# A two-layer attention and MLP kernel: twelve copies out of PSUM go from ScalarE to VectorE

## The chip, the cores and the metric

The kernel runs on one core of a Trainium2 chip. The metric is the device time of one execution in microseconds, and the figure quoted is the median of the runs. A profile is one execution recorded by the hardware profiler; its times count from the start of the recorded span. Names of engines in the profile: PE is TensorE (PEld its weight loads), DVE is VectorE, ACT is ScalarE, POOL is GpSimd, and SP is SyncE, which issues most transfers.

## The reference

The input is one sequence of 2048 tokens with 256 features, all in fp32. Four steps follow one another, each added to its input:

```python
x = x + attn_a(layernorm(x), Wq, bq, Wk, bk, Wv, bv, Wo, bo)  # 16 heads of 16, 4 key heads, rotary angles
x = x + ffn(layernorm(x), gate_W_packed, gate_scales, up_W_packed, up_scales, down_W_packed, down_scales)
x = x + attn_b(layernorm(x), Wq, Wk, Wv, Wo)                  # 16 heads, 16 key heads, no angles
x = x + ffn(layernorm(x), ...)                                # the same weights again
```

Both attentions are causal with a softmax over the keys. The MLP has 2048 inner features, weights of 4 bits with one scale for every 32 inputs, and computes

```python
gelu = jnp.tanh(0.7978845608028654 * (gate + 0.044715 * gate ** 3)) * gate * 0.5 + gate * 0.5
out = jnp.einsum('tn,hn->th', gelu * up, Wd)
```

## The kernel before, in words

The tokens are worked on in four blocks of 512 (`NB` = 4, each of `NT` = 4 tiles of 128). The program writes down the order of every engine's instructions itself: each engine carries out its own list strictly as written, and semaphores make it wait for what the others still owe it. `weave` and `blend` deal the steps of several lists among one another, and each step puts its instructions on all the engines that it needs, at that place of each engine's list.

**Attention.** `Attention.run` goes through 16 units, one for each block b of queries and group g of four heads. A unit computes scores, exponentials and value sums for its block (`value_steps`) while the maxima of the next unit are found (`max_steps`). The last unit, (3, 3), has no next unit. In its place it takes the steps in `beside`, which are the preparation of the MLP's first block (`Mlp.prep_steps(0)`: layer norm, four normalised tiles `xn`, and then four turns). In the first attention it also takes a third of the steps that dequantise the MLP's weights (`dequant_steps`), which are spread over most of the first attention's units.

In the inner loop of a unit PE puts two pairs of scores of a 128-key tile into `ps_s` (three buffers; L856 adds the negated maxima, L865 the scores), ACT turns them into exponentials `e` (L873), and PE multiplies those by the values into the one bank `ps_av` (L911). When a unit's sums are whole, `end` copies `ps_av` to `o` in SBUF (L942), and `divide` turns `o` on PE into the bank `ps_m` (L949) and has DVE divide by the row sums (L954, L957). `end` and `divide` of a unit are not carried out in that unit, but after the first and third steps of the next one, so that `end` of unit (3, 2) stands near the start of the last unit. `end` of unit (3, 3) stands after the last unit's steps, and its `divide` among the first MLP products.

**The MLP's first block.** `turn(i)` in `Mlp.prep_steps` transposes the tile `xn` number i on PE (two 128x128 transposes, L1102) into `ps_m`, of which there is one buffer only, and copies the result to its place in `xnT` (L1103, 128x256). The next use of `ps_m` waits for that copy. The first MLP products (L1126) need all four places of block 0's `xnT`. The same function prepares blocks 1 to 3 during the MLP itself.

**Dequantising.** A piece of weights has six steps: `load` (a transfer of the codes by SP and eight of the scales issued by POOL, L339; two buffers each), `lowest` (POOL copies the low byte of each code, L344, one buffer), two of `move` (three small DVE operations each, L355 to L361) and two of `scaled` (one DVE operation each, L370). For the four pieces of the down weights `scaled` ends in a store to DRAM by SP (`wd_kept`, L399, from the one-buffer tile `dq_d`), and the MLP loads that whole again as `wd` (L1118).

Of the kernel before, what the change touches and what calls it, by code (L numbers as in the profile page):

```python
# [27 lines left out]
NG = NH // 4  # L28
# [3 lines left out]
NB = S // TB  # L32
# [48 lines left out]
def tile_hybrid_layers(  # L81
# [25 lines left out]
    nc = tc.nc  # L107
# [20 lines left out]
    def ps_m():  # L128
        return psum.tile([P, 512], F32, tag="m", name="ps_m")
# [158 lines left out]
    def layernorm_steps(xb, held):  # L288


        def one(i):
            if i == 0:
                held["sums"] = small.tile([P, NT, 6], F32, tag="stats", name="stats")
                held["mv"] = small.tile([P, NT, 2], F32, tag="mv", name="mv")
            nc.vector.bn_stats(held["sums"][:, i, :], xb[:, i, :])
            nc.vector.bn_aggr(held["mv"][:, i, :], held["sums"][:, i, :])

        def root():
            ve = small.tile([P, NT], F32, tag="ve", name="ve")
            nc.vector.tensor_scalar(ve, held["mv"][:, :, 1], EPS, None, ALU.add)  # L300
            rstd = small.tile([P, NT], F32, tag="rstd", name="rstd")
            nc.gpsimd.tensor_tensor(rstd, ve, neg_half, ALU.pow)
            held["stats"] = (held["mv"], rstd)

        return [lambda i=i: one(i) for i in range(NT)] + [root]

    def normed(xb, i, stats):
        mv, rstd = stats
        xn = small.tile([P, D], F32, tag="xn", name="xn", bufs=4)
        nc.vector.tensor_scalar(  # L310
            xn, xb[:, i, :], mv[:, i, 0:1], rstd[:, i : i + 1], ALU.subtract, ALU.mult
        )
        return xn

    def new_xnT():
        return pre.tile([P, 2, TB], F32, tag="xnT", name="xnT", bufs=2)
# [94 lines left out]
    class Attention:  # L411
# [433 lines left out]
        def value_steps(self, b, g):  # L845
# [3 lines left out]
            held = {"e": {}}  # L849
# [71 lines left out]
            def rest(n):  # L921

                kt, q0 = first + n, (n + 1) * P
                w = TB - q0
                if n == 0:
                    of = lambda j: held["e"][kt, j // 2][:, j % 2, :w]
                else:
                    of = lambda j: held["e"][kt][:, j % 2, (j // 2) * w : (j // 2 + 1) * w]
                product(kt, slice(q0, TB), of, n == NT - 2)
# [8 lines left out]
            def end():  # L938
                rest(1)
                rest(2)  # L940
                o = pre.tile([P, TB], F32, tag="o", name="o")
                nc.scalar.copy(o, held["av"])  # L942
                held["o"] = o

            def divide():
# [17 lines left out]
            for kt in range(first):  # L963
# [14 lines left out]
                (lambda: both_pairs(first + 2), lambda: rest(0)),  # L978
            ]
            return steps, end, divide  # L980

        def out_steps(self, b):
# [99 lines left out]
    class Mlp:  # L1082
# [6 lines left out]
        def prep_steps(self, b):  # L1089
            held = {}  # L1090

            def norm(i):
                held["xn", i] = normed(xt[b], i, held["stats"])

            def turn(i):
                if i == 0:
                    self.xnT[b] = new_xnT()

                xn = held["xn", i].rearrange("p (f two) -> p two f", two=2)
                pt = ps_m()  # L1100
                for c in range(2):
                    nc.tensor.transpose(pt[:, c * P : (c + 1) * P], xn[:, c, :], ident)  # L1102
                nc.scalar.copy(  # L1103
                    self.xnT[b][:, :, i * P : (i + 1) * P],
                    pt[:, : 2 * P].rearrange("p (c t) -> p c t", c=2),
                )

            return (
                layernorm_steps(xt[b], held) + [lambda i=i: norm(i) for i in range(NT)]
                + [lambda i=i: turn(i) for i in range(NT)]  # L1110
            )
# [165 lines left out]
```

## Time and profile before

| | us |
|---|---|
| median of 3 runs | 1792.84 (1791.84 to 1794.59) |
| the profiled execution | 1790.76 |
| its span, first to last instruction | 1789.0 |
| PE busy in it | 1709.7 (96%) |
| DVE busy | 1113.2 (62%) |
| ACT busy | 799.8 (45%) |
| POOL busy | 242.2 (14%) |
| last unit of the first attention | about 533 to 567 in the span |
| last unit of the second attention | about 1412 to 1447 in the span |

A line of a timeline gives start, duration, engine, line of the program, operation, output and input with their sizes, how many like instructions are merged into the line, and in brackets how long the engine sat idle before it and what ended that. Matmuls are pipelined, and a merged line's duration reaches a little into the next line's start. A line of the busy time by windows gives for each engine the busy time and the count of instructions, then the granted clock of PE (1.00 is full speed), the share of DMA busy and its rate.

### The profile page before, as it was taken

The page shows a single profiled execution, that of the slowest core. Times are in us where ns is not written, and L with a number is a line of the kernel's source. Part 1 is how long each engine was busy: PE and PEld are TensorE (multiplying, and loading weights), DVE is VectorE, ACT ScalarE, POOL GpSimd, SP SyncE. Part 2 cuts the span into 40 slices and gives each one's busy share as a digit, 9 for nine tenths or more (in the row PEclk, how much of TensorE's full clock was granted, in tenths as well). Part 3 has the DMA queues.
Part 4 walks back from the last instruction along what each step waited for, and adds up shares of the span by engine and source line. Part 5 has one row for each costly group of instructions (what it writes and reads, how often), then busy time and mean ns, then how long its engine had stood idle before and what let it go on. Part 6 is the DMA issues. An engine that isn't in the chain of part 4 may idle for free.

```text
span 1789.0 us, 30446 instructions
## 1 busy us (share of the span) xinstructions
PE 1709.7 (96%) x12814; PEld 934.3 (52%) x12829; DVE 1113.2 (62%) x1615; ACT 799.8 (45%) x1016; POOL 242.2 (14%) x476
## 2 busy tenths in 40 slices
PE   8888899899999999999998899999999999999999
PEld 4544454444443474656475445444444445565646
DVE  5667987887874626362645777777878535445352
ACT  2435556666666313131314455555666742222231
POOL 4312211201103102012101010000000001111010
PEclk9999999999999999999999999999999999999999
DMA  5321301310003000005006042032000100000000
GB/s 154 92 60 56 73 25 46 73 29 25 13 2 125 6 1 1 0 0 129 1 2 129 17 89 50 13 66 54 14 13 1 49 1 3 9 7 6 10 3 12
DMA packets 43129, 65.33 MB, mean 37 GB/s; under 512 B 14000, under 2 KB 21040, under 8 KB 42736
## 3 DMA queue, kind: packets, MB, share of 16 engines
q1 hardware_dynamic: 34352, 47.37, 9.2%
q0 software_dynamic: 7680, 15.48, 4.9%
q8 instruction: 101, 1.65, 0.4%
q10 hardware_dynamic: 960, 0.52, 0.1%
q14 instruction: 36, 0.29, 0.1%
HBM read 43.45 MB, written 17.83 MB: 34 GB/s over the span
## 4 chain that ended last, share of the span: by engine, by line
PE 57%; DVE 7%; ACT 3%; issue 1%; POOL 0%; ACTq 0%; DVEq 0%; POOLq 0%
PE ps_s L1126 24%; PE ps_m L1151 6%; PE ps_av L1151 6%; DVE mx L776 6%; PE ps_av L911 6%; PE ps_s L856 4%; PE ps_s L769 3%; PE ps_s L865 3%; ACT e L873 2%; PE ps_m L1002 1%; PE ps_m L501 1%; PE ps_s L501 1%; PE ps_s L757 1%; PE ps_m L636 0%; PE ps_m L1102 0%
## 5 line engine op out<-in xcount | busy, mean ns | idle before, releaser
L776 DVE TENSOR_REDUCE mx<-ps_s 128x2 f32<-128x1024 f32 (+3 forms) x576 | 650.2, 1160 | 198.2 <-PE ps_s L769 152.0
L873 ACT ACTIVATE e<-ps_s 128x1024 f32<-128x1024 f32 (+1 forms) x576 | 555.6, 977 | 378.4 <-PE ps_s L865 307.1
L911 PE MATMUL ps_av<-e,v 128*32 128x256 f32 (+3 forms) x4672 | 331.9, 376 | 0.1
L865 PE MATMUL ps_s<-qT,kT 64*128 64x512 f32 (+3 forms) x1664 | 329.3, 445 | 0.0
L769 PE MATMUL ps_s<-kT,qT 64*128 64x512 f32 (+3 forms) x1664 | 258.0, 364 | 30.5 <-DVE mx L776 16.2
L1126 PE MATMUL ps_s<-xnT,wg 128*128 128x512 f32 x512 | 240.9, 593 | 0.0
L1126 PE MATMUL ps_s<-xnT,wu 128*128 128x512 f32 x512 | 240.6, 592 | 0.0
L856 PE MATMUL ps_s<-mT,sel 64*128 64x512 bf16 (+3 forms) x1280 | 219.1, 354 | 19.9 <-DVE mx L776 8.4
L769 PEld LDWEIGHTS ps_s<-kT,qT 64*128 64x128 f32 x1664 | 141.8, 186 | 126.0 <-DVE mx L776 53.8
L856 PEld LDWEIGHTS <-sel 64*128 64x128 bf16 x1280 | 66.6, 93 | 230.9 <-issue 218.1
L1132 ACT ACTIVATE t<-ps_s 128x512 f32<-128x512 f32 x128 | 76.3, 596 | 244.2 <-PE ps_s L1126 243.9
L1135 ACT ACTIVATE t<-t 128x512 f32<-128x512 f32 x128 | 80.6, 629 | 198.8 <-DVE t L1134 198.8
L1134 DVE TENSOR_TENSOR t<-ps_s,t 128x512 f32<-128x512 f32 x128 | 88.1, 688 | 124.5 <-POOL t L1133 122.3
L911 PEld LDWEIGHTS ps_av<-e,v 128*32 128x32 f32 x4672 | 102.3, 109 | 113.9 <-issue 99.4
L1126 PEld LDWEIGHTS ps_s<-xnT,wu 128*128 128x128 f32 x512 | 97.3, 190 | 122.5 <-issue 122.5
L1133 POOL TENSOR_SCALAR t<-t 128x512 f32<-128x512 f32 x128 | 79.1, 618 | 534.5 <-ACT t L1132 534.0
L865 PEld LDWEIGHTS ps_s<-qT,kT 64*128 64x128 f32 x1664 | 149.2, 193 | 2.0
L1126 PEld LDWEIGHTS ps_s<-xnT,wg 128*128 128x128 f32 x512 | 95.1, 190 | 104.2 <-issue 102.5
L1136 DVE SCALAR_TENSOR_TENSOR t<-t,ps_s 128x512 f32<-128x512 f32 x128 | 88.1, 688 | 89.0 <-ACT t L1135 89.0
L1151 PE MATMUL ps_av<-wd,inter 128*128 128x256 f32 x512 | 114.4, 380 | 0.0
L1151 PE MATMUL ps_m<-wd,inter 128*128 128x256 f32 x512 | 114.1, 379 | 0.0
L1151 PEld LDWEIGHTS ps_av<-wd,inter 128*128 128x128 f32 x512 | 96.8, 190 | 16.9 <-issue 4.2
(153 smaller groups left out, 1103.5 us busy)
## 6 DMA issues: line engine op xcount, KB each, us to landing
qT<-h SPq DMA_DIRECT2D x248, 64.0 KB, 2.2
kT<-h POOLq DMA_DIRECT2D x88, 128.0 KB, 5.9
h<-high SPq DMA_DIRECT2D x24, 256.0 KB, 2.2
h<-low SPq DMA_DIRECT2D x24, 256.0 KB, 2.5
wd<-wd_kept SPq DMA_DIRECT2D x2, 2048.0 KB, 8.2
wd_kept<-dq_d SPq DMA_DIRECT2D x4, 512.0 KB, 2.7
out<-x SPq DMA_DIRECT2D x16, 128.0 KB, 1.7
x<-x SPq DMA_DIRECT2D x3, 512.0 KB, 7.7
```

Of the source, the lines that this page charges most:

```text
L769: nc.tensor.matmul(pt[:, r, at : at + keys.stop - keys.start], lhsT=self.qT[b, g][64 * r : 64 * r + 64, p, i * P : (i + 1) * P], rhs=self. ...
L776: nc.vector.tensor_reduce(to, pt, AX.X, ALU.max)
L856: nc.tensor.matmul(pt[:, r, at : at + queries.stop - queries.start], lhsT=sel[64 * r : 64 * r + 64, p, :], rhs=self.mT[b, g][64 * r : 64 * ...
L865: nc.tensor.matmul(pt[:, r, at : at + queries.stop - queries.start], lhsT=self.key_rows(kt // NT, g, p, r, keys), rhs=self.qT[b, g][64 * r ...
L873: nc.scalar.activation(e, pt, AF.Exp, scale=QK_SCALE)
L911: nc.tensor.matmul(held["av"][32 * j : 32 * j + 32, to], lhsT=self.vv[kt // NT][:, kt % NT, h * VW : h * VW + 32], rhs=of(j), start=openin ...
L1126: nc.tensor.matmul(pt[:, k, :], lhsT=w[:, c, fc * P : (fc + 1) * P], rhs=self.xnT[b][:, c, :], start=(c == 0), stop=(c == 1),)
L1133: nc.gpsimd.tensor_scalar(t, t, GELU_A, 1.0, ALU.mult, ALU.add)
L1134: nc.vector.tensor_tensor(t, gate, t, ALU.mult)
L1135: nc.scalar.activation(t, t, AF.Tanh, scale=GELU_C)
L1136: nc.vector.scalar_tensor_tensor(t, t, 1.0, gate, ALU.add, ALU.mult)
L1151: nc.tensor.matmul(po[:, :D], lhsT=inter[:, fc, i * P : (i + 1) * P], rhs=wd[:, fc, :], start=(fc == 0), stop=(fc == NFC - 1),)
```

## The change

Two copies get another engine, in some places. `end` (L942) uses VectorE in place of ScalarE for the units (3, 2) and (3, 3). `turn` (L1103) uses VectorE for block 0 and ScalarE, as before, for the others. Block 0 has four turns and there are two attentions and two MLPs, so eight copies of 128x256 and four of 128x512 change their engine. Their places among the steps stay the same, so each stands on VectorE's list between the operations that the neighbouring steps put there.

```diff
@@ value_steps, end()
                 rest(1)
                 rest(2)
                 o = pre.tile([P, TB], F32, tag="o", name="o")
-                nc.scalar.copy(o, held["av"])
+                late = (b, g) >= (NB - 1, NG - 2)
+                (nc.vector.tensor_copy if late else nc.scalar.copy)(o, held["av"])
                 held["o"] = o
@@ Mlp.prep_steps, turn(i)
                 for c in range(2):
                     nc.tensor.transpose(pt[:, c * P : (c + 1) * P], xn[:, c, :], ident)
-                nc.scalar.copy(
+                (nc.scalar.copy if b else nc.vector.tensor_copy)(
                     self.xnT[b][:, :, i * P : (i + 1) * P],
                     pt[:, : 2 * P].rearrange("p (c t) -> p c t", c=2),
                 )
```

One line is added, so the lines below L942 have numbers higher by one in the changed kernel (L1103 becomes L1104).

## The prediction

> **What bounds the kernel now.** I read the page's totals first, then the busy time by windows over the two stretches in which the changed lines run (the last unit of each attention), and then the timelines of each engine there.
>
> ```profile
> span 1789.0 us, 30446 instructions
> PE 1709.7 (96%) x12814; PEld 934.3 (52%) x12829; DVE 1113.2 (62%) x1615; ACT 799.8 (45%) x1016; POOL 242.2 (14%) x476
> PE 57%; DVE 7%; ACT 3%; issue 1%; POOL 0%; ACTq 0%; DVEq 0%; POOLq 0%
> core 0: us, PE busy (x) PEld busy (x) DVE busy (x) ACT busy (x) POOL busy (x), PEclk, DMA share, GB/s
> 533.00:567.00 34.00, 33.33 (x325) 12.86 (x318) 14.85 (x48) 29.83 (x36) 15.52 (x29) 1.00 0.27 86
> 1412.00:1447.00 35.00, 34.86 (x338) 13.52 (x331) 4.23 (x15) 31.31 (x39) 1.03 (x1) 1.00 0.17 61
> ```
>
> TensorE (PE) is busy for 96% of the span, so a change gains only where PE waits, and any new wait of PE is paid in full. In the two windows PE is busy for 33.33 of 34 us and 34.86 of 35. ScalarE (ACT) is nearly as full there, 29.83 and 31.31, so it looks like a second bound. Whether it is one shows in the timelines of ACT and of PE:
>
> ```profile
> 537.52 17.10 ACT L873 ACTIVATE e<-ps_s 128x1024 f32<-128x1024 f32 x17 [0.25 <-PE ps_s L865]
> 554.51 0.37 ACT L1103 COPY xnT<-ps_m 128x256 f32<-128x256 f32 x1
> 557.09 1.94 ACT L873 ACTIVATE e<-ps_s 128x1024 f32<-128x1024 f32 x2 [1.01 <-PE ps_s L865]
> ...
> 537.81 1.06 PE L911 MATMUL ps_av<-e,v 128*32 128x512 f32 x8
> 539.82 1.07 PE L911 MATMUL ps_av<-e,v 128*32 128x512 f32 x8
> 555.37 1.07 PE L911 MATMUL ps_av<-e,v 128*32 128x512 f32 x8
> 557.38 0.50 PE L1102 MATMUL ps_m<-ident,xn 128*128 128x128 f32 x2
> ```
>
> ACT runs 17 exponentials without a gap, yet PE goes through one key tile (eight value products, two pairs of scores) from 537.81 to 539.82, in 2.01 us, and takes the same 2.01 us from 555.37 to 557.38, where ACT has caught up and waits 1.01 us for PE. So ACT is late but does not hold PE: two exponentials take 1.94 us, PE's tile takes 2.01.
>
> Next, where the moved copies stand. The changed kernel's order of instructions on VectorE (DVE) is decided by the program's text. In the first attention DVE also dequantises the MLP's weights, and the four copies of the MLP's first block come late among that work: the first copy stands behind the first of the two L370 operations that the timeline shows at 561.41 (the third of the four pieces of the down weights).
>
> ```profile
> 553.42 0.50 PE L1102 MATMUL ps_m<-ident,xn 128*128 128x128 f32 x2
> 554.93 0.50 PE L1102 MATMUL ps_m<-ident,xn 128*128 128x128 f32 x2 [0.45 <-ACT xnT L1103]
> 560.85 0.48 PE L1102 MATMUL ps_m<-ident,xn 128*128 128x128 f32 x2 [0.18 <-DVE xn L310]
> ...
> 554.62 0.41 DVE L310 TENSOR_SCALAR xn<-x,mv,rstd 128x256 f32<-128x256 f32 x1
> 559.69 0.23 DVE L355 TENSOR_SCALAR dq_t<-dq_b 128x128 uint32<-128x128 uint32 x1 [4.66 <-POOL dq_b L344]
> 561.41 1.51 DVE L370 SCALAR_TENSOR_TENSOR dq_d<-dq_e,dq_s 128x512 f32<-128x512 fp8e4 x2
> ...
> 555.00 4.04 POOL L339 DMA_DIRECT2D dq_s<-down_s  x8 [3.67 <-DVE dq_d L370]
> 559.04 0.62 POOL L344 COPY dq_b<-dq_q 128x512 uint8<-128x512 uint8 x1
> ```
>
> PE turns the four blocks at 553.42, 554.93, 557.38 and 560.85, all into the one ps_m bank; each turn needs the copy of the one before. ACT makes that copy at 554.51. DVE can't: from 555.03 it waits in its own order for GpSimd (POOL), which issues eight loads of scales from 555.00 and copies the low bytes at 559.04 to 559.66.
>
> **The change part by part.**
>
> First attention, the first turned block. The removed copy ended at 554.88 (554.51 + 0.37) and PE's second turn began at 554.93. The new one waits for the L355, L357, L361, L310 and L370 work in front of it. Nothing in that chain waits for the PE work that the change delays: POOL's loads wait for DVE's L370 (554.02 + 0.69), POOL's byte copy follows them, DVE follows that. L370 starts at 561.41; the first of the two took 0.91 alone, with some 0.07 overlapped by its follower as between other neighbours, so the copy starts at about 562.25. DVE's 128x256 operations from PSUM take 0.42 (L957, att): ended at 562.67. PE restarts some 0.08 later, 562.75. The second turn is late by 562.75 - 554.93 = **7.8 us**. Behind it on PE, in order, stand all the scores and value products of the rest of the unit; nothing of PE's is free to go ahead. Bounds: 7.5 (the copy begins as soon as L370's usual 0.69 is over) and 8.1 (0.69 for the copy, DVE's 128x512 cast from PSUM in L624, in place of 0.42).
>
> The other three copies. From one turn to the next PE has 2.45 us (554.93 to 557.38) and 3.47 (557.38 to 560.85) of other work. Between copies one and two DVE has one L370 (0.69), between two and three L355, L357 and L361 (some 0.6), between three and four the same and another L370. All fit, so these copies follow the turns at once: 0. The L370 ahead of the fourth waits for a store of dq_d (2.7 us to landing, by the page's list of DMA issues); issued about 563.5 it lands about 566.3, before that point. Cover gone, it would cost up to 1.6, the wait that this operation shows today. The first MLP products, 5.87 us behind the last turn on PE (560.85 to 566.72), find their fourth copy done. Its old 0.18 wait for xn goes: -0.2. The last piece's store of wd_kept and the 2 MB load of wd behind it on SP's queue move from 569.70 to about 577 and take 7.7: landed by 585, where the first use of wd is at 628.6 today and is itself moved: 0. POOL issues all its loads before 559.04: 0.
>
> The clock. PE stands idle from about 554.5 to 562.75, some 8.2 us, more than anywhere in this trace. The rows nearest to it:
>
> ```profile
> 104.28 0.61 PE L1027 MATMUL ps_m<-nothing,sel 128*128 128x512 bf16 x1 [2.04 <-DVE att L957]
> 104.00:112.00 8.00, 7.31 (x62) 4.31 (x66) 4.00 (x9) 1.02 (x1) 0.00 (x0) 0.57 0.00 0
> ```
>
> After 2.04 us without a matmul the mean granted clock in the 8 us is 0.57, with 0.50 in each single microsecond inside: (1 - 0.57) / 0.5 x 8 = 6.9 us at half speed. By the same sum the window 80 to 88 (0.57) has 6.9 and 933 to 938 (0.66) has 3.4. PE is full once it resumes, so half of such a stretch is lost: 1.7 to 3.4 us; a part that falls into the wait itself is free. Bounds 0 and 3.4; I take 2.5, the middle of the two lengths seen, since a gap four times as long should not do better. The Trainium skill's page "TensorE: Matmul & The Clock Gate", in its Part 1, says that half rate sets in after one idle window of about 3.4 us and ends after one busy window, the windows running free. By it 2.04 us should not have sufficed, and the trace says it did; for 8 us of idling page and row agree, and the page alone would make the sum's term 1.7 to 3.4 as well.
>
> The two value sums, first attention. The unit before last's sum is copied by ACT at 533.93 for 0.58; DVE is free there from 529.6 to 535.35 and takes about 0.69 (L624). PE's L949 starts 0.55 after its last pair's begin (534.10 to 534.65), the same spacing as between a pair and value products (537.26 to 537.81), so it waits for nothing: 0, between -0.2 and +0.2. The last unit's sum (ACT at 566.86) is needed by L949 at 570.26, 3.4 us on: 0 on either engine, and the DVE work ahead of it is over by then.
>
> Second attention. DVE has nothing there between the four norms (done at 1421.2) and 1451.36, so its copies come at once, at 1432.7 and later. PE doesn't wait for ACT's copies there today: turns at 1432.21, 1434.65, 1437.10 and 1440.34 show no idle time. Gain 0. Bounds: +0.1, and -0.6 (ACT loses 0.58 + 4 x 0.38 = 2.1 us of work, but PE's only waits for ACT there are weight loads at 1445.4 to 1445.9, 1.1 us in sum, behind the last exponentials, where ACT was itself idle before).
>
> On copies out of PSUM there is a line in "VectorE: DVE Perf Modes", Specifications: ScalarE sits closer to PSUM, VectorE closer to SBUF. By the page alone the move is wrong for each of the twelve copies. The rows go the same way by little: 0.69 on DVE against 0.58 on ACT for 128x512, 0.42 against 0.38 for 128x256. Only the one copy that PE waits for counts, 0.04 in a sum of ten.
>
> **Sum**: 7.8 - 0.2 + 2.5 = +10.1 us. The profiled execution took 1790.76 (span 1789.0), so it becomes 1800.9; the runs' median before is 1792.84, 2.1 above the profiled one, and on it the sum gives **1802.9**.
>
> **The rivals.**
> - *The stall without the clock's part*: 7.6 only, 1800.4. For it: the half-speed stretch may begin and partly pass inside the wait. Against: it has to end after PE is busy again, and the three stretches seen last 3.4 or 6.9.
> - *More than the sum*: the L370 before the fourth copy still waits, or the half clock lasts 6.9 from the restart: 1.6 + 0.9 more, 1805.4.
> - *DVE is in time*: no difference (within 0.2%, 3.6 us). The first copy would have to end by 558.5, so POOL's byte copy would come 4 us earlier than its loads let it.
> - *Faster*: ACT's lag does hold PE, though modelled ends hide it. ACT loses 2.1 us in each last unit, at most 4.2 in sum, 1788.6. It decides if a tile of scores takes PE less than 2.01 us once ACT is freed, and only if the stall is not there. The 2.01 with ACT waiting speaks against it.
>
> That the change doesn't do what it says is out: four copies of block 0 and two sums per attention stand on DVE in the changed order, twelve in all, and other engines' orders are the same.
>
> **How the numbers follow.** Stall and clock 0.70, stall alone 0.18, more 0.05, in time 0.04, faster 0.03. Low: 7.5 - 0.2 - 0.6 and no clock loss give +6.7; high: 8.1 + 3.4 + 0.1 + 1.6 = +13.2. On the median, cut to eight in ten: 1799 to 1806, the runs' own spread of 2.75 among it. About 0.2% is what a measurement can tell: slower 0.93 (the first three), same 0.04, faster 0.03.
>
> **What would show it.** Right: the second L1102 of the first attention starts near 562.7 with 8 us of idle time released by the DVE copy, a granted clock near 0.5 for 3 to 7 us from within the wait, the first MLP product near 576.8, and the second attention's last unit as long as now. Wrong: a DVE copy before 556, no half clock, or tiles under 2.0 us in the second attention.

## The result and the profile after

The changed kernel takes 1800.55 us (median of 6 runs, 1796.30 to 1806.29) against 1792.47 (6 runs, 1789.72 to 1794.59): a ratio of 1.0051 with a 95% interval of 1.0038 to 1.0064, which is 6.8 to 11.5 us more. The change makes the kernel slower by half a percent. The profiled execution took 1800.95 us, its span 1799.1. The page's totals:

```profile
span 1799.1 us, 30444 instructions
PE 1715.0 (95%) x12814; PEld 936.8 (52%) x12829; DVE 1119.3 (62%) x1627; ACT 795.9 (44%) x1004; POOL 241.7 (13%) x476
PE 58%; DVE 7%; ACT 3%; issue 1%; POOL 0%; ACTq 0%; DVEq 0%; POOLq 0%
```

The work did move: DVE has 12 instructions and 6.1 us more, ACT 12 fewer and 3.9 us less. PE carries out the same 12814 matmuls but is busy for 5.3 us longer, and the rest of the span's 10.1 us is, on balance, idle time. Where both lie is seen in PE's own waits between 520 and 590 us (the columns are the total, the number of waits and the longest), in PE's timeline of the first attention's last unit, and in the busy time by windows around the wait:

```profile
PE ps_m L1103 <- DVE xnT L1104: 8.2, 1, 8.2
PE ps_m L991 <- DVE att L958: 1.1, 1, 1.1
```

```profile
553.65 0.50 PE L1103 MATMUL ps_m<-ident,xn 128*128 128x128 f32 x2
554.09 0.39 PE L856 MATMUL ps_s<-mT,sel 64*128 64x512 bf16 x2
554.13 0.58 PE L865 MATMUL ps_s<-qT,kT 64*128 64x512 f32 x2
562.93 0.70 PE L1103 MATMUL ps_m<-ident,xn 128*128 128x128 f32 x2 [8.22 <-DVE xnT L1104]
563.56 1.94 PE L911 MATMUL ps_av<-e,v 128*32 128x512 f32 x8
567.26 0.51 PE L1103 MATMUL ps_m<-ident,xn 128*128 128x128 f32 x2
567.70 1.06 PE L911 MATMUL ps_av<-e,v 128*32 128x512 f32 x8
570.50 0.51 PE L1103 MATMUL ps_m<-ident,xn 128*128 128x128 f32 x2
576.38 1.98 PE L1127 MATMUL ps_s<-xnT,wg 128*128 128x512 f32 x4
```

```profile
core 0: us, PE busy (x) PEld busy (x) DVE busy (x) ACT busy (x) POOL busy (x), PEclk, DMA share, GB/s
553.00:563.00 10.00, 1.78 (x15) 0.80 (x11) 5.05 (x15) 2.77 (x3) 5.34 (x10) 0.70 0.32 106
563.00:568.00 5.00, 5.00 (x24) 1.60 (x28) 1.65 (x6) 1.44 (x2) 0.00 (x0) 0.58 0.26 107
568.00:577.00 9.00, 8.96 (x128) 4.88 (x121) 2.99 (x8) 5.47 (x7) 0.00 (x0) 1.00 0.15 60
```

The second turn begins 9.28 us after the first (562.93 - 553.65); before it was 1.51. The eight value products after it take 1.94 us in place of 1.07 and the granted clock is 0.58; from 568 on all is as it was. The half clock adds up to (1 - 0.70) / 0.5 x 10 + (1 - 0.58) / 0.5 x 5 = 6.0 + 4.2 = 10.2 us, of which the first 6.0 fall into the wait. In shorter windows the clock is seen to fall at 557.0 and to rise at 567.2 (of the last window 0.2 us are at half rate):

```profile
555.00:557.00 2.00, 0.00 (x0) 0.00 (x0) 0.25 (x1) 0.84 (x1) 1.78 (x4) 0.99 0.64 231
557.00:558.00 1.00, 0.00 (x0) 0.00 (x0) 0.00 (x0) 0.00 (x0) 1.00 (x3) 0.50 0.87 235
566.00:567.00 1.00, 1.00 (x8) 0.36 (x4) 0.00 (x0) 0.44 (x1) 0.00 (x0) 0.50 0.00 0
567.00:568.00 1.00, 1.00 (x8) 0.47 (x10) 0.20 (x1) 1.00 (x2) 0.00 (x0) 0.90 0.00 0
```

From the first turn to the first MLP product PE takes 576.38 - 553.65 = 22.73 us, and 566.72 - 553.42 = 13.30 in the kernel before. This stretch of 9.43 us more is the measure used below. It is read inside one execution, the profiled one of each kernel, and what the clock does elsewhere in a run does not touch it.

DVE's timeline shows what stands ahead of the copy, and the first line ends at the time from which DVE waits for POOL:

```profile
554.85 0.41 DVE L310 TENSOR_SCALAR xn<-x,mv,rstd 128x256 f32<-128x256 f32 x1
559.91 0.23 DVE L355 TENSOR_SCALAR dq_t<-dq_b 128x128 uint32<-128x128 uint32 x1 [4.66 <-POOL dq_b L344]
561.63 0.90 DVE L370 SCALAR_TENSOR_TENSOR dq_d<-dq_e,dq_s 128x512 f32<-128x512 fp8e4 x1
562.46 0.41 DVE L1104 COPY xnT<-ps_m 128x256 f32<-128x256 f32 x1
562.79 0.68 DVE L370 SCALAR_TENSOR_TENSOR dq_d<-dq_e,dq_s 128x512 f32<-128x512 fp8e4 x1
563.67 0.42 DVE L1104 COPY xnT<-ps_m 128x256 f32<-128x256 f32 x1 [0.20 <-PE ps_m L1103]
```

The operand of the first copy was in `ps_m` from 554.15; DVE took it up 8.3 us later. In the second attention the four copies follow their turns at once, and from the first turn to the first MLP product PE takes 14.01 us before (1432.21 to 1446.22) and after:

```profile
1442.36 0.51 PE L1103 MATMUL ps_m<-ident,xn 128*128 128x128 f32 x2
1456.37 1.98 PE L1127 MATMUL ps_s<-xnT,wg 128*128 128x512 f32 x4
```

### The profile page after: what moved, and what is told of

The parts are those of the page before. It is cut to its first block, busy times and chain, and to the rows that moved or that the text cites. A ratio compares the mean times of both kernels' runs of the same rounds, so it can differ in the third digit from the quotient of the medians.

```text
span 1799.1 us, 30444 instructions
## 1 busy us (share of the span) xinstructions
PE 1715.0 (95%) x12814; PEld 936.8 (52%) x12829; DVE 1119.3 (62%) x1627; ACT 795.9 (44%) x1004; POOL 241.7 (13%) x476
## 4 chain that ended last, share of the span: by engine, by line
PE 58%; DVE 7%; ACT 3%; issue 1%; POOL 0%; ACTq 0%; DVEq 0%; POOLq 0%
PE ps_s L1127 24%; PE ps_m L1152 6%; PE ps_av L911 6%; PE ps_av L1152 6%; DVE mx L776 6%; PE ps_s L856 4%; PE ps_s L769 3%; PE ps_s L865 3%; ACT e L873 2%; PE ps_m L1003 1%; PE ps_m L501 1%; PE ps_s L501 1%; PE ps_s L757 1%; PE ps_m L1103 0%; PE ps_m L636 0%
```

## The experiments

The theory to be tested (*queue*): the loss comes from the first attention's turned copies, which stand in VectorE's order behind dequantising work, and from the half clock that PE's idling brings on. The first rival (*price per copy*): VectorE is the worse engine for copies out of PSUM, and the loss spreads over all twelve. A second: the slow stretch of PE has another cause than the idling. All runs are compared with the kernel before on the same chip.

**The sums alone.** The changed kernel with the turned blocks back on ScalarE:

```diff
-                (nc.scalar.copy if b else nc.vector.tensor_copy)(
+                nc.scalar.copy(
                     self.xnT[b][:, :, i * P : (i + 1) * P],
```

> Only the four copies of the value sums (128x512) are moved to VectorE, the turned blocks stay on ScalarE. Theory (queue: the loss is the first attention's turned copies standing behind dequantising on VectorE, plus the half clock that follows): within 1 us of the kernel before; the first attention's second turn follows the first by 1.5 us as before. Rival (price per copy: VectorE reads PSUM more slowly, so each of the twelve copies costs): a third of the copies and half of their bytes, so 3 to 4 us of the 8 us.

Measured: 1792.37 us (10 runs) against 1791.38 (19 runs), ratio 1.0003 (0.9991 to 1.0014). The stretch from the first turn to the first MLP product is 13.34 us (13.30 before). The four copies of 128x512 cost nothing that can be measured, although each takes 0.69 us on DVE and 0.58 on ACT.

**The first attention's turned blocks alone.** The kernel before with

```diff
-                nc.scalar.copy(
+                (nc.vector.tensor_copy if b == 0 and not self.last else nc.scalar.copy)(
                     self.xnT[b][:, :, i * P : (i + 1) * P],
```

> Only the four turned copies of the first attention are moved to VectorE, one third of the moved copies. Queue theory: the whole loss, 8 to 10 us against before, with a wait of about 8.2 us before the second turn and 3 to 7 us of half clock after PE resumes. Price per copy: about 2 us.

Measured: 1798.96 us against 1791.38, ratio 1.0048 (1.0033 to 1.0063). The stretch is 22.62 us. Four of the twelve copies bring the whole loss. PE's waits between 520 and 590 us in this kernel, and its second and third turn, which are 4.19 us apart (2.45 before; 4.33 in the changed kernel):

```profile
PE ps_m L1102 <- DVE xnT L1103: 8.3, 1, 8.3
```

```profile
561.27 0.70 PE L1102 MATMUL ps_m<-ident,xn 128*128 128x128 f32 x2 [8.27 <-DVE xnT L1103]
565.46 0.50 PE L1102 MATMUL ps_m<-ident,xn 128*128 128x128 f32 x2
```

**All but the first attention's turned blocks.** The changed kernel with

```diff
-                (nc.scalar.copy if b else nc.vector.tensor_copy)(
+                (nc.vector.tensor_copy if b == 0 and self.last else nc.scalar.copy)(
```

> As the changed kernel, but the first attention's four turned copies go back to ScalarE; the other eight copies stay on VectorE. Queue theory: within 1 us of before, no wait for a turned copy over 0.5 us. Price per copy: two thirds of the loss, about 5 us. If ScalarE's backlog held PE in the second attention after all, this kernel would be faster than before by 1 to 2 us.

Measured: 1789.13 us (10 runs) against 1791.38, ratio 0.9999 (0.9987 to 1.0012). The interval holds 1, so the 2 us between the medians tell no difference; but it would leave room for the gain of 1 to 2 us too. The stretches decide: 13.34 us in the first attention, 14.01 in the second, and the whole last unit of the second attention, from its first scores to the first MLP product, takes 33.61 us (1410.42 to 1444.03), as before (1412.61 to 1446.22). Eight of the twelve copies on DVE are neutral: no loss, and no gain from a relieved ACT either.

**The number of copies behind one another.** The kernel before with `b == 0 and not self.last and i >= 1`, and with `... and i == 3`, in the line of the second experiment, so that the last three or only the last of the four turned copies move.

> The first attention's second, third and fourth turned copies are moved, the first stays on ScalarE. Queue theory: the second turn is on time, the third (557.4 us before) waits for a copy behind the second L370 and starts near 563.3, so a wait of 5.9 us and less half clock than with four: 6 to 8 us slower. Price per copy: three quarters of the loss with four copies.

> Of all copies only the first attention's fourth turned copy is moved. On VectorE it stands behind an L370 that waits until 565.7 us for a store. Queue theory: the copy ends near 566.8 and the first MLP product, at 566.7 before, waits 0.1 to 0.3 us: no difference to be measured. Price per copy: some 2 us by the copies of E2 (a quarter of 8).

Measured, one run each: 1800.74 us with three, 1788.23 with one. The stretch is 20.50 us (+7.20) with three and 13.44 (+0.14) with one. PE's timeline with three copies moved:

```profile
555.31 0.51 PE L1102 MATMUL ps_m<-ident,xn 128*128 128x128 f32 x2 [0.45 <-ACT xnT L1103]
563.68 0.70 PE L1102 MATMUL ps_m<-ident,xn 128*128 128x128 f32 x2 [5.85 <-DVE xnT L1103]
```

And DVE's timeline with only the last one moved:

```profile
563.66 0.69 DVE L370 SCALAR_TENSOR_TENSOR dq_d<-dq_e,dq_s 128x512 f32<-128x512 fp8e4 x1 [1.57 <-DMA wd_kept<-dq_d]
564.27 0.42 DVE L1103 COPY xnT<-ps_m 128x256 f32<-128x256 f32 x1
```

The wait of 5.85 us was expected as 5.9. The half clock is there too: the fourth turn follows the third 4.72 us later, and 3.47 in the kernel before. A price in proportion to the copies would have given some 2.4, 7.1 and 9.4 us for one, three and four; measured are 0.1, 7.2 and 9.4. The three copies don't tell the two theories apart by their sum, only by the place and length of the wait; the one copy does. It has to wait too, 1.57 us behind a store, but ends at 564.69, about where PE comes to the first MLP product (564.83). So what a copy costs is decided by how late it ends against PE's need of it.

**Dequantising out of the way.** In `Attention.run`, in the kernel before and in the changed one:

```diff
-            room = [0 if n < NG else 9 if n + 1 == len(units) else 2 * (g < 3 or b + 1 == NB)
+            room = [0 if n < NG else 0 if n + 1 == len(units) else 2 * (g < 3 or b + 1 == NB)
```

> The kernel before with one number changed: the last unit of the first attention gets no share of the dequantising, the units ahead of it get it all. This is the base for the next run. Nothing in the queue theory sets its time exactly: VectorE gets some 10 us more work spread over eleven units where it is busy with maxima, so 0 to 6 us slower than before.

> The changed kernel with the same number changed, so that on VectorE nothing of the dequantising stands in front of the turned copies. Queue theory: the stall is gone, the second turn follows the first without a wait for the copy, and the time is within 1 us of the run before this one. Price per copy: 8 us above that run, as in the change itself.

Measured: with ACT's copies 1795.13 us against 1791.33, ratio 1.0024 (1.0010 to 1.0038); with DVE's copies 1794.60, ratio 1.0023 (1.0008 to 1.0038). The stretch is 14.03 us in both. Its greater length against 13.30 comes with another spacing of the turns (2.46 us from the first to the second, and 1.51 before). The line gives the work to nine units, not to eleven as was expected of it: `g < 3` in three blocks. DVE's timeline with its copies:

```profile
556.52 0.42 DVE L1104 COPY xnT<-ps_m 128x256 f32<-128x256 f32 x1 [11.47 <-PE ps_m L1103]
558.98 0.42 DVE L1104 COPY xnT<-ps_m 128x256 f32<-128x256 f32 x1 [2.03 <-PE ps_m L1103]
```

Now DVE waits for PE, not PE for DVE, and the very change that costs 9.4 us costs nothing. The dequantising in front is the cause. Moving it, though, costs 0.24% by itself, so this is no better kernel; no version tried is faster than the kernel before by more than the scatter of the runs.

**A busy wait.** The changed kernel with 34 matmuls of zeros ahead of the second turn, into a score buffer that nobody reads:

```diff
+                if i == 1 and b == 0 and not self.last:
+                    spare = ps_s()
+                    for _ in range(34):
+                        nc.tensor.matmul(
+                            spare[:, 0, :], lhsT=sel[:, 0, :], rhs=nothing, start=True, stop=True
+                        )
                 pt = ps_m()
```

> As the changed kernel, with 34 extra 128x512 matmuls of zeros into a spare score buffer ahead of the first attention's second turn (some 7.3 us of PE work whose result nobody reads), so that PE waits without being idle. If the half clock comes from the idling: full clock throughout, second to third turn 2.45 us (4.33 in the changed kernel), and the first MLP product 1.9 us earlier than in the changed kernel, about 7.5 us after its place in the kernel before. If the slow stretch has another cause (the DVE or DMA work of that time): 4.3 us again and no difference to the changed kernel.

Measured: 1799.12 us against 1791.38, ratio 1.0047 (1.0032 to 1.0062). The stretch is 20.91 us, 7.61 more than before and 1.82 less than in the changed kernel. PE's timeline and the busy time by windows in this kernel:

```profile
553.72 0.50 PE L1109 MATMUL ps_m<-ident,xn 128*128 128x128 f32 x2
554.72 7.51 PE L1104 MATMUL ps_s<-nothing,sel 128*128 128x512 bf16 x33
563.06 0.51 PE L1109 MATMUL ps_m<-ident,xn 128*128 128x128 f32 x2 [0.83 <-DVE xnT L1110]
565.51 0.51 PE L1109 MATMUL ps_m<-ident,xn 128*128 128x128 f32 x2
574.63 1.98 PE L1133 MATMUL ps_s<-xnT,wg 128*128 128x512 f32 x4
```

```profile
553.00:563.00 10.00, 9.17 (x47) 3.96 (x44) 5.01 (x15) 2.85 (x3) 5.36 (x10) 1.00 0.34 106
563.00:568.00 5.00, 4.94 (x46) 2.36 (x46) 3.27 (x11) 1.94 (x2) 0.00 (x0) 1.00 0.28 110
```

The copy comes at the same time (33 of the 34 matmuls have a record), but the clock stays at 1.00, and from the second to the third turn PE takes 2.45 us and not 4.33. All three kernels in which PE idles for 5.9 to 8.3 us at this place show a half-clock stretch that begins inside the wait (10.2 us with four copies, twice, and 6.8 with three); this one, in which it works instead, shows none. So the idling brought on the half clock, and it cost 1.8 us. The whole runs can't tell this kernel from the changed one; the stretch can.

## Why the prediction was right, point by point

The sum of +10.1 us stands against 9.43 measured in the stretch where it was placed, and against 8.1 between the medians (6.8 to 11.5 by the ratio's interval). The predicted 1802.9 lies 2.4 above the median: 0.7 of it is the sum's excess over the stretch, 0.4 the median of the kernel before (1792.84 of three runs, 1792.47 of six), and the other 1.3 is within the scatter of the medians. The range and the direction held.

- *The second turn late by 7.8 us*: 9.28 - 1.51 = 7.77. Each link came as worked out. With the whole trace 0.23 us later than the one before, the copy was put at 562.48 and began at 562.46, took 0.41 (0.42 taken from `att`), and PE went on 0.06 later.
- *The other three copies free, and 0.2 us of an old wait gone*: from the second turn to the third 4.33 us at the half clock, from the third to the fourth 3.24 (3.47 before), from the fourth to the MLP 5.88 (5.87). The L370 ahead of the fourth copy had no wait. Its cover gone was priced at up to 1.6; with the fourth copy alone on DVE the wait was there, 1.57, and cost 0.14, since PE needed the copy only then.
- *The clock, 2.5 us*: this is the term that was mis-sized. It measures 1.9 from the second turn to the third (4.33 - 2.45) and 1.8 by the busy wait. The step took the two lengths of half-clock stretches in the trace, 3.4 and 6.9 us, as running from about PE's restart. The stretch was longer than either, and than the 3 to 7 us named as a sign of being right: 10.2 us. But it began inside the wait, and only 4.2 us of it met work. The prediction named that a part inside the wait is free and left it out of its middle value. The Trainium skill's "TensorE: Matmul & The Clock Gate", Part 1, has half rate set in after an idle window of about 3.4 us and end after a busy one. Here the granted clock fell some 2.3 us after PE fell idle (at 557.0) and rose again 4.3 us after it resumed. The trace agrees with the release; the start, like the one after 2.04 us in the trace before, comes sooner than 3.4 us after the last matmul.
- *Nothing from the four sums and nothing from the second attention*: shown by the sums alone (ratio 1.0003) and by all but the first turned blocks (0.9999). The reading behind it, that ACT without a gap is late but does not hold PE, stands: freed of its copies ACT ran 18 exponentials in a row, and PE's tiles still took 2.01 us each (538.04 to 540.05).

```profile
537.75 18.09 ACT L873 ACTIVATE e<-ps_s 128x1024 f32<-128x1024 f32 x18 [0.31 <-PE ps_s L865]
538.04 1.07 PE L911 MATMUL ps_av<-e,v 128*32 128x512 f32 x8
540.05 1.07 PE L911 MATMUL ps_av<-e,v 128*32 128x512 f32 x8
```

- *The rule on PSUM*: the Trainium skill's "VectorE: DVE Perf Modes", Specifications, has ScalarE closer to PSUM. The copies took 0.41 to 0.43 us on DVE and 0.37 to 0.39 on ACT, 0.69 and 0.58 for the larger. These rows go the way of the rule, and it is not why the change lost.

The match of the profiled execution (1800.95, predicted 1800.9) is partly chance. Of the 10.1 us that its span grew by, 9.43 lie in the stretch; the other 0.7 come from the rest of the run, where the clock was at half rate for longer than in the trace before (some 24 us in place of 17; mean granted clock 0.991 against 0.995), and they happen to make up for the clock's term.

## What to carry to other kernels

Before a step goes to an engine with idle time, look at what stands in front of it in that engine's own order, and at what that in turn waits for: DVE was idle for 4.7 of the 8.2 us, yet not free. Here the wait on a bank with one buffer held up all the scores and value products behind it on PE for 8.2 us, so the price of a copy is how late it ends against PE's need, not how long it takes. And an engine that is busy without a gap may still not be what holds the one that matters; compare the time per tile where it is late and where it has caught up.

## What the runs showed that was not expected

Half-clock stretches came in lengths of 3.4, 6.8 and 10.2 us, and not in the same places from one profiled execution to the next. Two of the three in the trace before set in where PE had not idled for as much as 1 us at a time: at 80.2 after one wait of 0.89, and at 933.5 after waits of 0.51, 0.50 and 0.88 in the 4.2 us before it. So the long idling shown above is one way into half rate, and what else decides where a stretch begins stays open. The means of the granted clock in ten profiled executions reach from 0.990 to 0.999, which is (1 - 0.990) / 0.5 x 1799 = 36 us of half rate at one end and under 4 at the other. The kernel before alone spread from 1787.27 to 1797.91 us over the runs, and its time goes with the clock: of 19 runs on one chip the four with a mean of 0.991 took 1794.33 to 1794.67 us, the three with 0.996 or 0.998 took 1787.27 to 1787.54. That scatter is larger than several of the differences sought here; a stretch measured inside one execution told 0.14 and 1.8 us apart where medians could not.
